# Self-products of batch rows: two adjacent rows to a partition, five long pieces a row, and paired product rows in one VectorE instruction

## The chip, the cores and the metric

The kernel runs on one core of a Trainium2 chip; the other cores are idle. The metric is the device time of one execution in microseconds (us). Ten runs of the kernel before gave 1312.31 to 1312.87 us, with a median of 1312.55.

## What is computed

The input has 4096 batch rows of 256 float32 numbers. For each row the kernel writes the upper triangle of the outer product of the row with itself:

```python
dot = jnp.einsum('bi,bj->bij', inputs, inputs)
iu, ju = jnp.triu_indices(d)
return dot[:, iu, ju]
```

The triangle is written row by row: first x[0] times x[0:256], then x[1] times x[1:256], and so on down to x[255] times itself. In this text a *product row* i is x[i] times x[i:256], with 256 - i numbers. An output row has 256 x 257 / 2 = 32,896 numbers, or 131,584 bytes; the output has 538.97 MB, the input 4.19 MB. There is one multiplication for each number that is stored.

## The kernel before, in words

The batch rows lie on the 128 partitions. A *group* is 512 batch rows: four tiles (t = 0 to 3, `GROUP`) of 128 rows, so that partition p holds rows p, 128 + p, 256 + p and 384 + p of the group, and there are 8 groups. At the start SP issues eight loads of 512 KB (L61), one for each group; each brings 128 x 4 rows of 1 KB. The input stays on the chip.

The output row is cut at multiples of 128 columns into 16 pieces (`CHUNKS`, `chunk_borders`) of 2,048 columns, the last of 2,176. The outer loop runs over the groups (L64), the inner one over the pieces (L66). For each piece a tile `o` is taken from a pool of 4 buffers (L53, L67); it holds the piece for all four rows of a partition. `runs` lists the stretches of product rows that fall into the piece. A stretch of up to 64 numbers (`SHORT`) takes one tensor_tensor on VectorE for the four rows together (L71), whose second operand is the factor, repeated along the stretch. A longer stretch takes four instructions, one for each row: three tensor_scalar on VectorE (L86) and one activation on ScalarE (L84), with the factor as their scale. Then SP issues one store of the piece for the 512 rows (L87): 4 MB, in packets of 8,192 bytes, one for each row.

Every engine works through its queue in the order in which the program issues. The framework puts in the waits: the first writer of a tile waits until the store that last read this buffer has landed (all 16 DMA engines have added to its semaphore), and SP's store waits for the last instruction of VectorE and of ScalarE on the tile. Two writers of one tile that overlap are ordered as well: if they stand on one engine, the later one waits for a semaphore that the earlier one raises. In the kernel before no two instructions on one tile are ordered in this way. A DMA of 128 partitions is spread over 16 DMA engines, which work through their shares at their own pace. 7383 instructions are in the profile; instructions themselves come into the engines' queues through a DMA queue (q14 in the profile).

Of the kernel before, what the change touches and what calls it, by code (L numbers as in the profile page):

```python
# [1 line left out]

# [4 lines left out]

F32 = mybir.dt.float32
AF = mybir.ActivationFunctionType
ALU = mybir.AluOpType  # L10

P = 128
UNIT = 128      # columns: chunk borders are multiples of it, 512 bytes in HBM
CHUNKS = 16     # pieces that an output row is cut into
GROUP = 4       # batch tiles of 128 rows that are computed and stored together
SHORT = 64      # runs up to this length take one instruction for the whole group


def chunk_borders(width: int) -> list[int]:
    units = width // UNIT  # L20
    borders = [units * c // CHUNKS * UNIT for c in range(CHUNKS)]
    return borders + [width]


def runs(d: int, lo: int, hi: int):
    """The runs of output columns [lo, hi) with one first factor: (i, j, column, length), for
    x[i] * x[j : j + length]. Row i of the upper triangle has j from i on."""
    at = 0
    for i in range(d):
        a, b = max(at, lo), min(at + d - i, hi)  # L30
        if a < b:
            yield i, i + a - at, a, b - a
        at += d - i


@with_exitstack
def kernel(
    ctx: ExitStack, tc: tile.TileContext, x: bass.AP, out: bass.AP
):
    """out[n, :] = the upper triangle, row by row, of the outer product of x[n] with itself.  # L40

    Batch rows lie on the partitions. The input stays on chip; the output is made chunk by chunk
    and each chunk goes out in one store while the next ones are computed."""
    nc = tc.nc
    n, d = x.shape
    width = out.shape[1]
    assert n % (P * GROUP) == 0 and width == d * (d + 1) // 2 and width % UNIT == 0
    groups = n // (P * GROUP)
    borders = chunk_borders(width)
    widest = max(b - a for a, b in zip(borders, borders[1:]))  # L50

    xpool = ctx.enter_context(tc.tile_pool(name="x", bufs=1))
    opool = ctx.enter_context(tc.tile_pool(name="o", bufs=4))  # L53

    x_in = x.rearrange("(g t p) d -> g p t d", t=GROUP, p=P)
    x_out = out.rearrange("(g t p) c -> g p t c", t=GROUP, p=P)

    xs = []
    for g in range(groups):
        xt = xpool.tile([P, GROUP, d], F32, tag=f"x{g}", name=f"x{g}")  # L60
        nc.sync.dma_start(xt, x_in[g])  # L61
        xs.append(xt)

    for g in range(groups):  # L64
        xt = xs[g]
        for c, (lo, hi) in enumerate(zip(borders, borders[1:])):  # L66
            o = opool.tile([P, GROUP, widest], F32, tag="o", name=f"o_{g}_{c}")  # L67
            for i, j, col, length in runs(d, lo, hi):
                a = col - lo
                if length <= SHORT:  # L70
                    nc.vector.tensor_tensor(  # L71
                        o[:, :, a : a + length],
                        xt[:, :, j : j + length],
                        xt[:, :, i : i + 1].to_broadcast([P, GROUP, length]),
                        ALU.mult,
                    )
                    continue
                for t in range(GROUP):
                    dst = o[:, t, a : a + length]
                    src = xt[:, t, j : j + length]  # L80
                    factor = xt[:, t, i : i + 1]
                    # Of four such instructions one goes to the Scalar engine.
                    if t == GROUP - 1:
                        nc.scalar.activation(dst, src, AF.Copy, scale=factor)  # L84
                    else:
                        nc.vector.tensor_scalar(dst, src, factor, None, ALU.mult)  # L86
            nc.sync.dma_start(x_out[g][:, :, lo:hi], o[:, :, : hi - lo])  # L87


# [1 line left out]
_INS = ["r_inputs"]  # L91
_OUTS = [((4096, 32896), "float32")]


# [20 lines left out]
```

## Time and profile before

| What | Before |
|---|---|
| Time, median of 10 runs | 1312.55 us |
| Time of the profiled execution | 1312.31 us |
| Its span, first to last event | 1310.5 us |
| VectorE (DVE) busy | 1117.1 us, 5272 instructions |
| ScalarE (ACT) busy | 506.2 us, 1553 instructions |
| DMA, mean over the span | 415 GB/s |
| Stores | 120 of 4096 KB and 8 of 4352 KB |
| Median from issue to landing of a 4096 KB store | 31.5 us |
| Last compute instruction ends | 1287.9 us |

Busy time is the time in which at least one instruction of the engine was under way; instructions can overlap on an engine, so "mean ns of one" times the count can be more than the busy time. The slices divide the span into 40 equal parts; a digit is the busy share of a part in tenths. "Idle before" is the time for which an engine did nothing ahead of an instruction, with what ended that wait behind the arrow. A row of the table of stretches gives, for a stretch of the span in us, its length, the busy time and the number of instructions of VectorE, ScalarE and GpSimd, the granted clock, the mean busy share of the 16 DMA engines and the rate at which they moved bytes. A share can be slightly above 1, because packets of one DMA engine overlap.

### The profile page before, as it was taken

To read this page: it belongs to the slowest core of one execution; us is meant where nothing else is said; L and a number is where in the kernel's file an instruction comes from. 1 tells how busy PE (TensorE), PEld (TensorE's weight loads), DVE (VectorE), ACT (ScalarE), POOL (GpSimd) and SP (SyncE) were. 2 spreads that over 40 slices of the span, in tenths; PEclk is the share of its full clock that TensorE was granted. 3 is DMA by queue.
4 is the path that set the end of the run, shared out by engine and by line. 5 is a ranking of instruction groups with operands and counts; after the bars stand their busy time and mean duration, and the time that the engine had idled before them with its cause. 6 is when DMAs were issued, how large, how long until landed. Compare 5 with 4: busy or idle time off the path is not lost.

```text
span 1310.5 us, 7383 instructions
## 1 busy us (share of the span) xinstructions
DVE 1117.1 (85%) x5272; ACT 506.2 (39%) x1553; POOL 0.2 (0%) x4
## 2 busy tenths in 40 slices
DVE  8889977899788997789977899778996789977893
ACT  5345234442344523345333443334433443334430
POOL 0000000000000000000000000000000000000000
DMA  9999999999999999999999999999999999999996
GB/s 370 427 427 422 419 420 419 419 419 420 418 420 419 420 418 420 418 420 419 419 419 419 419 419 419 418 419 419 420 418 419 418 420 419 420 418 420 419 420 276
DMA packets 71865, 543.64 MB, mean 415 GB/s; under 512 B 2176, under 2 KB 6272, under 8 KB 6272
## 3 DMA queue, kind: packets, MB, share of 16 engines
q1 hardware_dynamic: 71808, 543.17, 100.0%
q14 instruction: 57, 0.47, 0.1%
HBM read 4.19 MB, written 538.97 MB: 414 GB/s over the span
## 4 chain that ended last, share of the span: by engine, by line
DMA 54%; DVE 43%; issue 0%; DVEq 0%; SPq 0%
DMA out_dram<-o 54%; DVE o L86 34%; DVE o L71 9%; DMA x<-in_r_inputs_dram 0%; DVEq L71 0%; SPq L87 0%; DVEq L86 0%; DVEq L111 0%
## 5 line engine op out<-in xcount | busy, mean ns | idle before, releaser
L86 DVE TENSOR_SCALAR o<-x 128x256 f32<-128x256 f32 (+44 forms) x4656 | 993.1, 329 | 110.6 <-DMA out_dram<-o 106.4
L84 ACT ACTIVATE o<-x 128x105 f32<-128x105 f32 (+59 forms) x1552 | 504.9, 416 | 762.7 <-DMA out_dram<-o 754.7
L71 DVE TENSOR_TENSOR o<-x 128x112 f32<-128x112 f32 (+51 forms) x616 | 141.4, 382 | 60.1 <-DMA out_dram<-o 60.1
L84 ACT ACT_TABLE_LOAD x1 | 1.3, 1283 | 0.7 <-PEq L102 0.7
L102 POOL MEMSET const-bfloat16-1.0<- 128x1 bf16 x1 | 0.1, 101 | 0.0
L102 POOL MEMSET const-uint8-127<- 128x1 uint8 x1 | 0.1, 101 | 0.0
L102 POOL MEMSET const-float32-0.0<- 128x1 f32 x1 | 0.1, 98 | 0.2 <-issue 0.2
L102 POOL MEMSET const-float32-1.0<- 128x1 f32 x1 | 0.1, 98 | 0.0
## 6 DMA issues: line engine op xcount, KB each, us to landing
out_dram<-o SPq DMA_DIRECT2D x120, 4096.0 KB, 31.5
out_dram<-o SPq DMA_DIRECT2D x8, 4352.0 KB, 22.6
x<-in_r_inputs_dram SPq DMA_DIRECT2D x8, 512.0 KB, 8.4
```

Of the source, the lines that this page charges most:

```text
L71: nc.vector.tensor_tensor(o[:, :, a : a + length], xt[:, :, j : j + length], xt[:, :, i : i + 1].to_broadcast([P, GROUP, length]), ALU.mult,)
L84: nc.scalar.activation(dst, src, AF.Copy, scale=factor)
L86: nc.vector.tensor_scalar(dst, src, factor, None, ALU.mult)
L102: nc = _bacc.Bacc("TRN2", target_bir_lowering=False, num_devices=1)
```

## The change

- **Rows and partitions.** Partition p now holds 32 adjacent batch rows, 32p to 32p + 31, in one input tile. It is loaded in three parts: the first two rows of every partition (256 KB), the rest of the first half, and the second half. The outer loop runs over 16 groups of two adjacent rows a partition (`REPEAT`), 256 batch rows in all.
- **Pieces.** The output row is cut into 5 pieces (`PIECES`) of 6,528 or 6,592 columns, at multiples of 64. A piece of two rows is a tile of 128 x 2 x 6,592 numbers, from a pool of 3 buffers. One store takes it out, 6.7 MB, one run of 26 KB for each row. The very first piece is cut in four (`FIRST`), each with a store of its own: 512, 1,024, 2,048 and 2,944 columns.
- **Instructions.** For a product row (or a stretch of one) there are three ways on VectorE: "each", one tensor_scalar for each of the two rows; "all", one tensor_tensor for both rows; "two", one tensor_tensor for both rows and two product rows that follow each other. In the last, the second product row is taken as long as the first, one number too long, and the number too many is overwritten by the product row after it. `vector_ops` chooses by a formula for the times.
- **Order.** `interleave` cuts VectorE's part of a piece in two halves and issues one instruction of either half in turn.
- **The split.** `split` gives the first product rows of a piece to ScalarE, one activation for each batch row, until VectorE's part fits in a budget of 1.08 ns for each number of a partition, or ScalarE has more to do than VectorE. In the first piece the budget is 0, so that the two engines share it by time.

The diff, with runs of empty lines closed up:

```diff
--- before.py
+++ after.py
@@ -10,81 +10,159 @@
 ALU = mybir.AluOpType
 
 P = 128
-UNIT = 128      # columns: chunk borders are multiples of it, 512 bytes in HBM
-CHUNKS = 16     # pieces that an output row is cut into
-GROUP = 4       # batch tiles of 128 rows that are computed and stored together
-SHORT = 64      # runs up to this length take one instruction for the whole group
+UNIT = 64
+REPEAT = 2
+PIECES = 5
+BUDGET = 1.08
+FIRST = [512, 1536, 3584]
 
 
-def chunk_borders(width: int) -> list[int]:
-    units = width // UNIT
-    borders = [units * c // CHUNKS * UNIT for c in range(CHUNKS)]
-    return borders + [width]
+def even_borders(lo: int, hi: int, pieces: int) -> list[int]:
+    units = (hi - lo) // UNIT
+    return [lo + units * c // pieces * UNIT for c in range(pieces)] + [hi]
 
 
-def runs(d: int, lo: int, hi: int):
-    """The runs of output columns [lo, hi) with one first factor: (i, j, column, length), for
-    x[i] * x[j : j + length]. Row i of the upper triangle has j from i on."""
-    at = 0
+def runs(d: int, lo: int, hi: int) -> list:
+
+    found, at = [], 0
     for i in range(d):
         a, b = max(at, lo), min(at + d - i, hi)
         if a < b:
-            yield i, i + a - at, a, b - a
+            found.append((i, i + a - at, a, b - a))
         at += d - i
+    return found
+
+def vector_ops(block: list) -> list:
+
+    ops, k = [], 0
+    while k < len(block):
+        i, j, at, n = block[k]
+        two = k + 2 < len(block) and i == j
+        each = REPEAT * (130 + 0.52 * n)
+        together = 68 + 1.046 * REPEAT * n - (34 if two else 0)
+        if each <= together:
+            ops.append(("each", block[k]))
+        elif two:
+            ops.append(("two", block[k]))
+            k += 1
+        else:
+            ops.append(("all", block[k]))
+        k += 1
+    return ops
+
+def interleave(block: list) -> list:
+
+    half, at = 0, sum(n for *_, n in block) / 2
+    while half < len(block) and at > 0:
+        at -= block[half][3]
+        half += 1
+    a, b = vector_ops(block[:half]), vector_ops(block[half:])
+    return [op for k in range(max(len(a), len(b))) for ops in (a, b) for op in ops[k : k + 1]]
+
+def vector_time(block: list) -> float:
+    t = 0.0
+    for way, (i, j, at, n) in vector_ops(block):
+        if way == "each":
+            t += REPEAT * (130 + 0.52 * n)
+        else:
+            t += 68 + 1.046 * REPEAT * n * (2 if way == "two" else 1)
+    return t
+
+def split(block: list, budget: float) -> int:
+
+    scalar, k = 0.0, 0
+    while k < len(block):
+        scalar += REPEAT * (184 + 0.837 * block[k][3])
+        if vector_time(block[k:]) <= budget or scalar > vector_time(block[k + 1 :]):
+            break
+        k += 1
+    return k
+
+def window(ap: bass.AP, free: list) -> bass.AP:
+    return bass.AP(ap.tensor, ap.offset, [list(ap.ap[0]), *free])
 
 
 @with_exitstack
 def tile_self_products_kernel(
     ctx: ExitStack, tc: tile.TileContext, x: bass.AP, out: bass.AP
 ):
-    """out[n, :] = the upper triangle, row by row, of the outer product of x[n] with itself.
 
-    Batch rows lie on the partitions. The input stays on chip; the output is made chunk by chunk
-    and each chunk goes out in one store while the next ones are computed."""
+
     nc = tc.nc
     n, d = x.shape
     width = out.shape[1]
-    assert n % (P * GROUP) == 0 and width == d * (d + 1) // 2 and width % UNIT == 0
-    groups = n // (P * GROUP)
-    borders = chunk_borders(width)
-    widest = max(b - a for a, b in zip(borders, borders[1:]))
+    assert n % (P * REPEAT) == 0 and width == d * (d + 1) // 2 and width % UNIT == 0
+    groups = n // (P * REPEAT)
+    borders = even_borders(0, width, PIECES)
+    slot = max(b - a for a, b in zip(borders, borders[1:]))
 
     xpool = ctx.enter_context(tc.tile_pool(name="x", bufs=1))
-    opool = ctx.enter_context(tc.tile_pool(name="o", bufs=4))
+    opool = ctx.enter_context(tc.tile_pool(name="o", bufs=3))
 
-    x_in = x.rearrange("(g t p) d -> g p t d", t=GROUP, p=P)
-    x_out = out.rearrange("(g t p) c -> g p t c", t=GROUP, p=P)
+    x_in = x.rearrange("(p r) d -> p (r d)", p=P)
+    x_out = out.rearrange("(p g r) c -> g p r c", p=P, r=REPEAT)
 
-    xs = []
-    for g in range(groups):
-        xt = xpool.tile([P, GROUP, d], F32, tag=f"x{g}", name=f"x{g}")
-        nc.sync.dma_start(xt, x_in[g])
-        xs.append(xt)
+
+    total = n // P * d
+    xt = xpool.tile([P, total + 1], F32, name="x")
+    nc.vector.memset(xt[:, total:], 0.0)
+    cuts = [0, REPEAT * d, total // 2, total]
+    for a, b in zip(cuts, cuts[1:]):
+        nc.sync.dma_start(xt[:, a:b], x_in[:, a:b])
 
     for g in range(groups):
-        xt = xs[g]
         for c, (lo, hi) in enumerate(zip(borders, borders[1:])):
-            o = opool.tile([P, GROUP, widest], F32, tag="o", name=f"o_{g}_{c}")
-            for i, j, col, length in runs(d, lo, hi):
-                a = col - lo
-                if length <= SHORT:
+            o = opool.tile([P, REPEAT, slot], F32, tag="o", name=f"o_{g}_{c}")
+            first = g == c == 0
+            cuts = [lo, *(FIRST if first else []), hi]
+            for a, b in zip(cuts, cuts[1:]):
+                block = runs(d, a, b)
+                k = split(block, 0.0 if first else BUDGET * REPEAT * (b - a))
+                for i, j, at, length in block[:k]:
+                    for r in range(REPEAT):
+                        row = (g * REPEAT + r) * d
+                        nc.scalar.activation(
+                            o[:, r, at - lo : at - lo + length],
+                            xt[:, row + j : row + j + length],
+                            AF.Copy,
+                            scale=xt[:, row + i : row + i + 1],
+                        )
+                row = g * REPEAT * d
+                for way, (i, j, at, length) in interleave(block[k:]):
+                    at -= lo
+                    if way == "each":
+                        for r in range(REPEAT):
+                            row_r = row + r * d
+                            nc.vector.tensor_scalar(
+                                o[:, r, at : at + length],
+                                xt[:, row_r + j : row_r + j + length],
+                                xt[:, row_r + i : row_r + i + 1],
+                                None,
+                                ALU.mult,
+                            )
+                        continue
+                    m = 2 if way == "two" else 1
                     nc.vector.tensor_tensor(
-                        o[:, :, a : a + length],
-                        xt[:, :, j : j + length],
-                        xt[:, :, i : i + 1].to_broadcast([P, GROUP, length]),
+                        o[:, :, at : at + m * length].rearrange("p r (m l) -> p r m l", m=m),
+                        window(xt[:, row + j :], [[d, REPEAT], [1, m], [1, length]]),
+                        window(xt[:, row + i :], [[d, REPEAT], [1, m], [0, length]]),
                         ALU.mult,
                     )
-                    continue
-                for t in range(GROUP):
-                    dst = o[:, t, a : a + length]
-                    src = xt[:, t, j : j + length]
-                    factor = xt[:, t, i : i + 1]
-                    # Of four such instructions one goes to the Scalar engine.
-                    if t == GROUP - 1:
-                        nc.scalar.activation(dst, src, AF.Copy, scale=factor)
-                    else:
-                        nc.vector.tensor_scalar(dst, src, factor, None, ALU.mult)
-            nc.sync.dma_start(x_out[g][:, :, lo:hi], o[:, :, : hi - lo])
+                nc.sync.dma_start(x_out[g][:, :, a:b], o[:, :, a - lo : b - lo])
 
 
 # ---- launch: one core; inputs and outputs as the reference has them ----
```

## The prediction

> **What bounds the kernel now.** I read the page first: busy time, the forty slices, the DMA queues, the costliest groups.
>
> ```profile
> DVE 1117.1 (85%) x5272; ACT 506.2 (39%) x1553; POOL 0.2 (0%) x4
> ...
> DMA  9999999999999999999999999999999999999996
> GB/s 370 427 427 422 419 420 419 419 419 420 418 420 419 420 418 420 418 420 419 419 419 419 419 419 419 418 419 419 420 418 419 418 420 419 420 418 420 419 420 276
> ...
> q14 instruction: 57, 0.47, 0.1%
> ...
> L86 DVE TENSOR_SCALAR o<-x 128x256 f32<-128x256 f32 (+44 forms) x4656 | 993.1, 329 | 110.6 <-DMA out_dram<-o 106.4
> L71 DVE TENSOR_TENSOR o<-x 128x112 f32<-128x112 f32 (+51 forms) x616 | 141.4, 382 | 60.1 <-DMA out_dram<-o 60.1
> ```
>
> The 16 DMA engines are busy in every slice but the last, and VectorE's idle time ends with the landing of a store: it waits for buffers. The stores bound the kernel, at 428 GB/s early and 419 for the rest. Then the busy time per stretch, at both ends:
>
> ```profile
> 5.00:10.00 5.00, 5.00 (x21) 5.00 (x14) 0.00 (x0) 1.00 0.97 319
> ...
> 20.00:100.00 80.00, 71.30 (x320) 32.78 (x98) 0.00 (x0) 1.00 1.01 428
> ...
> 140.00:1280.00 1140.00, 983.01 (x4633) 442.03 (x1358) 0.00 (x0) 1.00 1.01 419
> ...
> 1300.00:1305.00 5.00, 0.00 (x0) 0.00 (x0) 0.00 (x0) 1.00 0.08 33
> 1305.00:1310.50 5.50, 0.00 (x0) 0.00 (x0) 0.00 (x0) 1.00 0.05 21
> ```
>
> The last two columns are the share of the DMA engines and GB/s. For the last 10 us the share is about 1/16: one engine of sixteen is late and alone sets the end. The landing records say the same: the lag of the last of 16 engines grows from 2 us to 10-12 us. I put it down to the 57 instruction packets of 8 KB: 7383 instructions to 57 packets is 130 a packet, VectorE's 5404 in the program fill 42, and 36 store packets took about 655 ns, twice the usual 316. 42 x 0.24 us = 10 us.
>
> Last, the timeline, for the price of one VectorE instruction:
>
> ```profile
> 4.12 6.35 DVE L86 TENSOR_SCALAR o<-x 128x256 f32<-128x256 f32 x24 [4.12 <-DMA x<-in_r_inputs_dram]
> ...
> 55.45 0.29 DVE L71 TENSOR_TENSOR o<-x 128x128 f32<-128x128 f32 x1 [2.24 <-DMA out_dram<-o]
> ...
> 65.24 0.33 DVE L71 TENSOR_TENSOR o<-x 128x164 f32<-128x164 f32 x1 [2.08 <-DMA out_dram<-o]
> ...
> 1274.65 13.21 DVE L71 TENSOR_TENSOR o<-x 128x256 f32<-128x256 f32 x64
> ```
>
> In a row, 64 tensor_tensor of together 8,320 elements take 13.21 us: 68 ns + 1.04 ns an element from start to start. Alone, 128 and 164 elements last 0.29 and 0.33 us: 158 ns + 1.04 an element. So the next one starts some 90 ns before its forerunner's recorded end. A tensor_scalar costs 129 ns + 0.52 an element (23 starts in 6.0 us at 252 elements).
>
> **What the Trainium skill says.** "DMA: Bandwidth & Descriptors", Why small descriptors are slow: a fixed overhead per packet; the trace agrees in kind, see the packet law below. The same page, Latency and other measured facts: a pitch of 4 MiB between partitions halved the rate of HBM copies and 4 KiB more restored it; no run here shows such a pitch. "Perfetto Trace Analysis", Per-engine timelines: the recorded end includes the acknowledgement of the writes, while the next instruction may start its prefetch earlier; the 90 ns agree. "VectorE: DVE Perf Modes", The DRAIN you can't avoid: a semaphore after each instruction cost nothing extra. That test added increments; for a wait on the instruction just ahead the trace argues otherwise.
>
> **The change, part by part.**
>
> *Stores.* Per row and piece, 2,048 columns (8,192 B, 65,536 packets) become about 6,579 (26.3 KB, some 20,500 packets). At 419.4 GB/s an 8 KB packet takes 8,192 x 16 / 419.4 = 312.5 ns on its engine. The loads' 1 KB packets moved 319 GB/s at a share of 0.97, or 49.8 ns. A line through both is 12 ns + 0.0367 ns/B, and gives 431 GB/s at 26.3 KB. The packet records of 8,704 B against 8,192 B (335 and 316 ns) give a steeper slope, 0.038, hardly a fixed part, and 420.5. I take 425, near the middle, and keep both ends. 538.97 MB at 425 is 1268 us.
>
> *Loads.* 4.19 MB in packets of 2 to 16 KB at 428 instead of about 330 GB/s: 9.8 us; from 2.1 us on they end at 11.9, against about 15 now. The first store needs only 512 columns, so it is queued behind the loads in time.
>
> *Instructions and the late engine.* The built program has 3,034 VectorE instructions instead of 5,404: 24 packets for 42, and the late engine lags 24 x 0.24 = 5.7 us, not 10.
>
> *VectorE.* It gets 1,326 tensor_scalar of 310,574 elements (171 + 161 us) and 1,635 tensor_tensor of 648,150 (111 + 674): 1118 us, as now. ScalarE falls to 786 instructions, about 231 us at 184 ns + 0.84 an element: it can bind nothing. But waits are added. Overlapping writes (a pair of rows writes one column too many) are ordered, and the interleaving was to put a stranger between them. In the built order 1,071 waits on VectorE's own semaphore name the instruction directly ahead: the tracker orders tiles by their whole interval over both batch rows. Behind such a wait stands all of VectorE's queue, then SP's store. Its price is not in the trace; bounded: the end of the forerunner (158 + 1.04n), 11 ns to the semaphore (the records of VectorE's own updates), and from there to the start 25 ns, as at the first instruction after its load landed, or 123 ns, as where a wait instruction of its own stands ahead. Less the 68 of the unhindered sequence: 126 or 224 ns. From below, zero, if the wait is met anyway. I take 126, since 1,055 of the waits sit on the instruction itself: 135 us. VectorE then needs 1118 + 135 = 1253 us for 1268 us of stream. The cover is thin: of five pieces the last three have 236, 345 and 429 such waits in 16 groups, so 15.9, 16.8 and 17.5 us a piece against 15.9 of stream; the first two (13.5 and 14.5) pay it back.
>
> *Three buffers, larger.* A piece may be computed while one store runs and one waits. In the first group there is no lead yet, and stores 3 and 5 come late by some 4 us in sum (the chain of VectorE reaches piece 5 at about 78, the DMA wants it at 76).
>
> *The sum.* 11.9 + 1268 + 4 + 5.7 + 0.5 (last landing) = 1290 us of span. VectorE's own chain: 4.1 to the first data + 1253 + 8 (64 separate waits of about 0.1, and others) + 18 for the last store = 1283, below it. The profiled execution took 1312.31 for a span of 1310.5, so 1.8 more: 1292 us. The median of the runs, 1312.55, is 0.24 above that one execution.
>
> **The rivals.**
>
> *The chain of waits becomes the bound (slower).* VectorE-bound, the span is 1148 + 1.071 us for each ns of a wait. From 154 ns on that passes 1313.4, which is slower by over 0.2%; at the middle between 126 and 224, 175 ns, 1335 and so 1337 us; at 224, 1390. For it: 1,071 waits in a row, and a margin of 15 us. Against: the wait is on the instruction itself, where 25 ns was seen.
>
> *Packet length doesn't pay.* If the 7 ns more than early (309 to 316 in the records) grow with bytes, the stream stays at 419 to 420.5: 1282 to 1285, in sum 1304 to 1307 of span, 1306 to 1309 us. For it: the 8,704 B packets. Against: the 1 KB loads.
>
> *All of it is per packet, and waits cost little.* 431 GB/s: 1250.5 + 11.9 + 3 + 5.7 + 0.5 = 1272, or 1273 us.
>
> *The pitch.* Partitions are now 32 x 131,584 B apart, 4 MiB + 16 KiB, where 131,584 B stood. By the skill the odd KiB should save it. A rate under 417 is already slower than before: (1313.4 - 22) us for 538.97 MB.
>
> **How the numbers follow.** Forecast (1276 to 1304 us) 0.58; chain of waits from 154 ns on 0.18; length doesn't pay 0.12; all per packet 0.05; pitch 0.07. About 0.2% is what a measurement of this kernel can tell from no change. Faster: 0.58 + 0.05 + 0.09 of the second rival + 0.02 of the first at its lower edge = 0.74; within: 0.07; slower: 0.19. The range runs from the 1272 of the per-packet case to the 1337 of the chain at 175 ns; outside lie about 0.07 of the chain, 0.05 of the pitch and 0.02 below.
>
> **What would show it.** GB/s of 425 in the slices from the fourth on; 1 KB packets gone, and a last stretch with a share of 1/16 that lasts 5 to 6 us; VectorE's idle time named by its own semaphore, some 130 us, and starts of tensor_tensor 194 ns + 1.04 an element apart; little left of its waits for stores. Wrong it would be with DMA slices under 9 in the middle (VectorE-bound), or with a rate of 419 or less at full share.

## The result, and the profile after

The changed kernel takes 1283.36 us (median of 8 runs, 1283.29 to 1283.49), against 1312.68 us for the kernel before in the same sessions: a ratio of 0.9776, 95% interval 0.9768 to 0.9785, or 29.3 us less. The profiled execution has a span of 1281.6 us. The forecast was 1292, with a range of 1272 to 1337.

The page of the changed kernel, the same parts as were shown of before and the shares of the chain that ended last:

```profile
DVE 1219.2 (95%) x2962; ACT 235.4 (18%) x787; POOL 0.2 (0%) x4
...
DMA  9999999999999999999999999999999999999999
GB/s 383 405 395 432 422 432 435 421 432 422 432 422 422 433 422 432 435 419 423 433 431 425 426 428 422 432 434 421 422 427 427 435 420 434 422 433 422 432 422 395
...
q14 instruction: 32, 0.26, 0.1%
...
DVE 95%; issue 3%; DVEq 0%
DVE o L159 69%; DVE o L150 26%; DVEq L159 0%
...
L159 DVE TENSOR_TENSOR o<-x 128x2 f32<-128x2 f32 (+51 forms) x1635 | 915.3, 573 | 37.7 <-DVE o L159 0.5
...
L150 DVE TENSOR_SCALAR o<-x 128x216 f32<-128x216 f32 (+6 forms) x1326 | 366.2, 355 | 3.5 <-DMA x<-in_r_inputs_dram 2.4
```

(The chain that ended last is the work followed back from the last instruction to what released it each time.) In the kernel before, its shares were:

```profile
DMA 54%; DVE 43%; issue 0%; DVEq 0%; SPq 0%
```

Two readings. The rate has risen from 419 to some 427 GB/s. And VectorE no longer waits for a single store: of 166.5 us of such idle time nothing is left, and the chain that ended last runs through VectorE for 95% of the span, and no longer through the stores. VectorE has become the bound, though the DMA slices are all 9: here a DMA queue that is only just fed looks as busy as one that is full.

The stretches of the changed kernel (length, busy time and count of VectorE, ScalarE, GpSimd, clock, DMA share, GB/s):

```profile
5.00:10.00 5.00, 5.00 (x22) 5.00 (x14) 0.00 (x0) 1.00 1.02 429
...
20.00:100.00 80.00, 78.11 (x196) 14.21 (x48) 0.00 (x0) 1.00 0.95 407
...
140.00:1255.00 1115.00, 1080.39 (x2629) 198.97 (x672) 0.00 (x0) 1.00 1.00 427
...
1260.00:1265.00 5.00, 0.99 (x6) 0.00 (x0) 0.00 (x0) 1.00 1.00 427
...
1275.00:1281.60 6.60, 0.00 (x0) 0.00 (x0) 0.00 (x0) 1.00 0.61 260
```

From 5 to 10 us, while the loads run, the rate is 429 GB/s instead of 319. Between 20 and 100 us the stream falls to 407: the first group, in which VectorE has no lead. At the end there is no stretch with 1/16 of the engines: in the landing records the 16 engines of a store land within 1.9 us of each other from the first store to the last. That fits an engine that catches up whenever the queue runs short; in experiments 2 and 3 below, where VectorE is held up too, they stay within 1.7 us, and in the kernels with multiplications whose stream is the bound (before, and experiments 1, 4 and 5) one engine falls behind by 7 us or more.

Last, single forms of line 159 in the changed kernel (busy us and mean ns of one, idle us before them, all of one form together):

```profile
L159 DVE TENSOR_TENSOR o<-x 128x804 f32<-128x804 f32 x16 | 16.0, 999 | 0.5
...
L159 DVE TENSOR_TENSOR o<-x 128x360 f32<-128x360 f32 x32 | 17.1, 534 | 1.1
```

804 elements last 999 ns, 360 last 534: within 5 ns of 158 ns + 1.04 an element, the time of an instruction alone. The idle time ahead is 0.5 us for 16, 1.1 us for 32, or 34 ns each. So they follow each other at 192 ns + 1.04 an element, not at the 68 of the unhindered sequence: 124 ns for a wait, where 126 was forecast. As an instruction counts as busy until its recorded end, most of this shows as busy time (1219 us, where the unhindered sum is 1118) and only 37.7 us of it as idle time. The waits can be counted in the trace: 1,070 of VectorE's instructions start within 100 ns after the end of the one ahead, 34 ns in the median; the others start before that end, or after a longer pause (17 of them).

### The profile page after: what moved, and what is told of

It reads as the page before. It is cut to its first block, busy times and chain, and to the rows that moved or that the text cites. A ratio compares the mean times of both kernels' runs of the same rounds, so it can differ in the third digit from the quotient of the medians.

```text
span 1281.6 us, 4091 instructions
## 1 busy us (share of the span) xinstructions
DVE 1219.2 (95%) x2962; ACT 235.4 (18%) x787; POOL 0.2 (0%) x4
## 3 DMA queue, kind: packets, MB, share of 16 engines
HBM read 4.19 MB, written 538.97 MB: 424 GB/s over the span
## 4 chain that ended last, share of the span: by engine, by line
DVE 95%; issue 3%; DVEq 0%
DVE o L159 69%; DVE o L150 26%; DVEq L159 0%
## 5 line engine op out<-in xcount | busy, mean ns | idle before, releaser
L159 DVE TENSOR_TENSOR o<-x 128x2 f32<-128x2 f32 (+51 forms) x1635 | 915.3, 573 | 37.7 <-DVE o L159 0.5
L138 ACT ACTIVATE o<-x 128x197 f32<-128x197 f32 (+25 forms) x786 | 234.1, 390 | 1005.3 <-DMA out_dram<-o 778.6
L150 DVE TENSOR_SCALAR o<-x 128x216 f32<-128x216 f32 (+6 forms) x1326 | 366.2, 355 | 3.5 <-DMA x<-in_r_inputs_dram 2.4
L138 ACT ACT_TABLE_LOAD x1 | 1.3, 1283 | 0.7 <-PEq L180 0.7
```

What stands on the lines that cost most here:

```text
L138: nc.scalar.activation(o[:, r, at - lo : at - lo + length], xt[:, row + j : row + j + length], AF.Copy, scale=xt[:, row + i : row + i + 1],)
L150: nc.vector.tensor_scalar(o[:, r, at : at + length], xt[:, row_r + j : row_r + j + length], xt[:, row_r + i : row_r + i + 1], None, ALU.mult,)
L159: nc.vector.tensor_tensor(o[:, :, at : at + m * length].rearrange("p r (m l) -> p r m l", m=m), window(xt[:, row + j :], [[d, REPEAT], [1, ...
```

## The experiments

My theory after the result: VectorE's waits on the instruction directly ahead set the end, and the stream by itself would allow less. The rival: the stream sets it, and the waits lie beside it.

**1. The same instructions, another view of the output.** Most of the waits come from how the output of line 159 is written: through a rearranged view, which by the prediction is tracked as one interval over both batch rows. This run writes it as a plain slice.

```diff
-                        o[:, :, at : at + m * length].rearrange("p r (m l) -> p r m l", m=m),
+                        o[:, :, at : at + m * length],
```

> The changed kernel with the output of the tensor_tensor written as a plain slice instead of a rearranged view: same instructions and operands, but only 304 instead of 1,071 of VectorE's waits on itself name the instruction directly ahead. Theory (VectorE's chain of waits sets the end): VectorE sheds some 767 x 124 ns = 95 us, waits for stores again, and the time falls to what the stream allows, 1275 to 1279 us. Rival (the stream of stores already sets the end, the waits lie beside it): within 1 us of 1283.4.

Measured: 1277.72 us (0.9732 of before, 0.9717 to 0.9746), 5.6 less than the changed kernel. The shares of the chain that ended last, and the two groups of VectorE:

```profile
DMA 54%; DVE 43%; issue 1%; DVEq 0%; SPq 0%
...
L159 DVE TENSOR_TENSOR o<-x 128x660 f32<-128x660 f32 (+50 forms) x1635 | 831.8, 574 | 66.5 <-DMA out_dram<-o 56.0
...
L150 DVE TENSOR_SCALAR o<-x 128x225 f32<-128x225 f32 (+5 forms) x1326 | 347.9, 344 | 22.8 <-DMA out_dram<-o 20.1
```

The waits of this run (engine and line, for whom, us in total, times, longest):

```profile
DVE o L159 <- DMA out_dram<-o: 56.0, 41, 2.1
DVE o L150 <- DMA out_dram<-o: 20.1, 13, 1.6
```

and its stretches:

```profile
20.00:100.00 80.00, 79.35 (x211) 14.17 (x48) 0.00 (x0) 1.00 1.01 433
100.00:1200.00 1100.00, 1017.16 (x2609) 198.41 (x672) 0.00 (x0) 1.00 1.00 430
...
1265.00:1270.00 5.00, 0.00 (x0) 0.00 (x0) 0.00 (x0) 1.00 0.47 200
1270.00:1275.00 5.00, 0.00 (x0) 0.00 (x0) 0.00 (x0) 1.00 0.05 21
```

VectorE waits for stores again, 76 us, the stream runs at 430, the chain that ended last runs mostly through the stores, and the late engine is back at the end. A tensor_tensor lasts as long as before (574 and 573 ns in the mean), but only 304 instructions are left with a gap of some 34 ns ahead. Busy time and idle time other than for stores and loads fall from 1258 to 1165 us in sum: 93 us for 767 waits, or 122 ns each. The theory holds: with most of the waits gone the stream is the bound, and it ends 5.6 us before VectorE's chain did.

**2. Without the interleaving.**

```diff
-                for way, (i, j, at, length) in interleave(block[k:]):
+                for way, (i, j, at, length) in vector_ops(block[k:]):
```

> The changed kernel without the interleaving of the two halves of a piece: 1,193 waits on the instruction directly ahead instead of 1,071. Theory (chain of waits sets the end): up to 122 x 124 ns = 15 us more, 1290 to 1298 us. Rival (stream sets the end): within 1 us of 1283.4.

Measured: 1296.26 us, 12.9 more than the changed kernel for 122 more waits, 106 ns each. The edit also pairs the rows a little differently, with 32 instructions fewer (1,603 tensor_tensor for 1,635); at the 68 ns that one costs unhindered they would save 2.2 us, and with these the price is 124 ns a wait, by this estimate. What is added to the chain arrives at the end nearly whole: the rival is out.

**3. Less work for VectorE.**

```diff
-BUDGET = 1.08
+BUDGET = 1.0
```

> The changed kernel with a budget of 1.00 instead of 1.08: 86 us of multiplications move from VectorE (1118 to 1031) to ScalarE (226 to 372). Theory A (VectorE's own chain is the whole of it): VectorE ends well ahead, the stream sets the end, 1275 to 1279 us. Theory B (the view by whole intervals also orders ScalarE's and VectorE's writes to one piece, so that VectorE waits for ScalarE's longer share): slower, 1300 to 1320 us.

Measured: 1319.74 us, 1.0052 of the kernel before (1.0037 to 1.0066). Taking 86 us of work from the engine that is the bound costs 36 us. One of its waits, which the changed kernel doesn't have:

```profile
DVE o L159 <- ACT o L138: 138.2, 46, 6.7
```

ScalarE and VectorE touch no common number. But if the rearranged view counts as everything between its first and its last byte, a tensor_tensor over both batch rows covers ScalarE's share of the second row too, and waits for ScalarE. Theory A falls, and B has the sign and the size right; the next run tests whether it is the view.

**4. Both.** The plain slice and the budget of 1.00.

> Plain output slice and budget of 1.00 together. If the stream sets the end once the waits are gone, 1275 to 1279 us, as with the plain slice alone; if VectorE still sets it there, some 5 us or more below the plain slice alone.

Measured: 1276.33 us (0.9721 of before, 0.9705 to 0.9737), the fastest kernel of this study: 7.0 us below the changed one, 36.6 below the one before in its session. Its waits for stores:

```profile
DVE o L159 <- DMA out_dram<-o: 114.3, 45, 3.5
DVE o L150 <- DMA out_dram<-o: 46.9, 20, 3.6
```

Against experiment 1 it is only 1.4 less, with VectorE's waits for stores at 161 us instead of 76: the stream is the bound in both. Against experiment 3 the one edit of the view is worth 43.4 us, and no wait of VectorE for ScalarE is left. That shows the view as the cause of the waits on ScalarE too. How the framework compares the bytes behind a view is not shown by these runs; they show that the waits come with the view and go with the plain slice.

**5. No pairs.** Is the pairing of product rows, from which the overlaps come, worth having?

```diff
-        two = k + 2 < len(block) and i == j
+        two = False
```

> The changed kernel with the pairing of product rows switched off: every tensor_tensor takes one product row. No two writes of VectorE overlap, so none of its instructions waits on another; VectorE has 1113 us of work as before the edit, ScalarE 393 instead of 226, and VectorE's instructions go from 2,961 to 4,545. If the waits alone kept the changed kernel from the stream's time: 1278 to 1281 us (the stream's 1277 and up to 3 us for 12 more instruction packets on the late engine). If the pairing itself was worth something: slower than 1283.

Measured: 1286.90 us, 3.5 more than the changed kernel, not 2 to 5 less. VectorE waits for stores (125 us), the stream runs at 430, and no instruction of VectorE is left with a gap of some 34 ns ahead: the waits are gone and the stream is the bound. The end shows what was missed:

```profile
1265.00:1270.00 5.00, 0.00 (x0) 0.00 (x0) 0.00 (x0) 1.00 0.66 285
1270.00:1275.00 5.00, 0.00 (x0) 0.00 (x0) 0.00 (x0) 1.00 0.09 37
1275.00:1280.00 5.00, 0.00 (x0) 0.00 (x0) 0.00 (x0) 1.00 0.06 26
1280.00:1285.00 5.00, 0.00 (x0) 0.00 (x0) 0.00 (x0) 1.00 0.04 16
```

For 15 us one DMA engine of sixteen is still at work. In the landing records of the last store 13 engines end within 0.2 us, one 15.7 us after the first; in experiment 1 that is 7.6. The first engine is only 1.0 us later than in experiment 1, so 8.1 of the 9.2 us between the two are the late engine. There are 48 instruction packets instead of the 32 of the changed kernel and of experiment 1, 16 more and not 12. The pairing is worth its fewer instructions, not its VectorE time, if it is the instruction packets that make the engine late; experiment 7 tests that.

**6. The stores alone.** Five kernels with no loads and no multiplications, only the stores of resident buffers, in two row layouts and three packet lengths. Their stream starts only after the buffers have been filled, at 37 us with 8 KB packets, 42 with 26 KB and 47 with 44 KB, so the rates are compared between lengths, not the times. The core of the edit, against the changed kernel:

```diff
-            for a, b in zip(cuts, cuts[1:]):
-                block = runs(d, a, b)
...
+            o = os[k % BUFS]
+            nc.vector.memset(o[:, :, 0:1], float(k))
+            nc.sync.dma_start(x_out[g][:, :, lo:hi], o[:, :, : hi - lo])
```

> Stores alone, loads and multiplications left out: rows, pieces and buffers as in the kernel before (8 KB packets, 128 rows between a partition's rows). 419 to 421 GB/s in the middle slices if the stream by itself is what the kernel before ran at; no engine late at the end, since there are hardly any instructions.

> Stores alone, loads and multiplications left out: adjacent rows, but 8 KB packets of 4 rows and 4 buffers. If only packet length matters, 419 to 421 GB/s as in the kernel before; if the new row layout helps or hurts by itself, another rate.

> Stores alone: loads and multiplications are left out (one column of a buffer is set before each store). Rows, pieces and buffers as in the changed kernel: 26 KB packets, adjacent rows. If the packet law holds half way (some 8 ns a packet), 428 to 431 GB/s in the middle slices; if length doesn't pay, 419 to 421; if the pitch of 4 MiB + 16 KiB hurts, below 417.

> Stores alone, loads and multiplications left out: 26 KB packets in the row layout of the kernel before (128 rows between a partition's two rows). If only the packet's length matters, 430 GB/s as with adjacent rows; if the pitch of 4 MiB + 16 KiB costs something at this length, more than 431.

> Stores alone, loads and multiplications left out: one row a partition and store, in three pieces of 44 KB. By the packet law (12 to 14 ns a packet and 0.0367 ns a byte) 432 GB/s in the middle slices, 2 more than with 26 KB; if the gain ends at some length, 430.

Measured, in the same stretch of each run (length, VectorE, GpSimd, clock, share, GB/s). 8 KB in the rows of before:

```profile
100.00:1200.00 1100.00, 6.76 (x109) 0.00 (x0) 1.00 1.01 419
```

8 KB in adjacent rows:

```profile
100.00:1200.00 1100.00, 6.76 (x109) 0.00 (x0) 1.00 1.01 419
```

26 KB in adjacent rows:

```profile
100.00:1200.00 1100.00, 4.20 (x70) 0.00 (x0) 1.00 1.00 430
```

26 KB in the rows of before:

```profile
100.00:1200.00 1100.00, 4.20 (x70) 0.00 (x0) 1.00 1.00 430
```

and 44 KB in adjacent rows:

```profile
100.00:1200.00 1100.00, 5.01 (x85) 0.00 (x0) 1.00 1.00 432
```

Within one length the times can be compared too: 1327.77 and 1327.78 us for the two layouts at 8 KB, 1300.77 and 1300.76 at 26 KB. The 44 KB run starts its stream last and still ends first, at 1299.29. The layout is worth nothing, the length of the packet what there is. It isn't the number of stores: there are 128 at 8 KB, 80 at 26 KB, and 96 at 44 KB, which is faster with more of them. 8,192 bytes at 419 GB/s are 313 ns an engine, 26,317 at 430 are 979, 43,861 at 432 are 1624: about 12 ns a packet and 0.0367 ns a byte to within 3 ns, the line of the prediction drawn from 1 KB and 8 KB.

**7. Instructions as packets.** The 8 KB stores in the rows of before, with 5,248 tiny VectorE instructions added, in two placements. First 41 after each store, on a tile of their own:

```diff
-EXTRA = 0
+EXTRA = 41
...
             for e in range(EXTRA):
                 nc.vector.memset(busy[:, e % 8 : e % 8 + 1], float(e))
```

Then 41 ahead of each store, on its buffer:

```diff
-            nc.sync.dma_start(x_out[g][:, :, lo:hi], o[:, :, : hi - lo])
             for e in range(EXTRA):
-                nc.vector.memset(busy[:, e % 8 : e % 8 + 1], float(e))
+                nc.vector.memset(o[:, e % 4, 1 + e // 4 : 2 + e // 4], float(e))
+            nc.sync.dma_start(x_out[g][:, :, lo:hi], o[:, :, : hi - lo])
```

> The run of the kernel before's stores alone with 5,248 tiny VectorE instructions added (41 after each store), which touch none of the stores' buffers. Theory (instruction packets delay one DMA engine): 41 more packets of 8 KB, 10 us more than without them, and a last stretch of 10 us with a DMA share of about 1/16. Rival (the late engine has another cause): no difference over 1 us.

> Stores alone of 8 KB packets, loads and multiplications left out, with 5,248 tiny VectorE instructions as before, but 41 of them ahead of each store on its buffer, so that they are spread over the whole run and not bunched at its start. Theory A (each instruction packet costs the late engine some 0.24 us, as worked out from the kernel before; bunching made it 0.5): 10 us over the 1327.8 us of the run without them. Theory B (it is the number of such instructions, however placed): 20 to 23 us over it.

Measured: 1350.57 us in the first placement, 22.8 over the run without them; 1339.92 in the second, 12.2 over it. In the first, the framework moved the tiny instructions forward, up to 219 between two stores, and the last of them ran at 316 us; in the second, each 41 wait for a buffer and are spread over the run. Both have 45 instruction packets instead of 4. The end of the run without them, where all engines are busy together until it is over:

```profile
1310.00:1320.00 10.00, 0.00 (x0) 0.00 (x0) 1.00 1.01 422
1320.00:1330.00 10.00, 0.00 (x0) 0.00 (x0) 1.00 0.41 173
```

The end of the spread run:

```profile
1325.00:1330.00 5.00, 0.00 (x0) 0.00 (x0) 1.00 0.09 36
1330.00:1335.00 5.00, 0.00 (x0) 0.00 (x0) 1.00 0.06 26
1335.00:1338.20 3.20, 0.00 (x0) 0.00 (x0) 1.00 0.04 16
```

One engine is late by 12 us, with hardly any computation in the kernel. In the landing records of the last store one engine comes 11.8 us after the first, where that is 0.7 without the tiny instructions. In the bunched run this lag has grown to 21 us by the store that lands at 271 us, and after the last tiny instruction it no longer grows. The packet records show where the time goes: in the spread run 40 of the 8 KB store packets took over 500 ns, 655 in the median, where 314 is usual, and 39 of the 45 instruction packets ran at the same time as one of these. It is the instruction packets that delay the engine. 12.2 us for 41 packets are 0.30 us each when spread, 0.56 when bunched. Theory A was right on the placement and 2 us low. Why a packet costs more when they are bunched was not settled.

## Why the prediction was right, and where it was wrong

- *The sum.* 1292 was forecast, 1283.4 measured, inside the range and on the right side, at 1.4 times the forecast gain. The error is 8.6 us, and not all of one kind: a stream that was put 15 us too long stood first in the sum, and the second sum, VectorE's, set the end. That the number came out as near as it did rests on the two sums having been 7 us apart.
- *The stream's rate: the step that failed.* "I take 425, near the middle": the stores alone run at 430, and so does the stream where VectorE's waits are gone. The line through 1 KB and 8 KB gives 978 ns for a 26 KB packet, where 979 were measured. The other end came from packets of 8,704 against 8,192 bytes, which differ by 19 ns; 1 ns more or less in that difference moves the fixed part of a packet by 16 ns. And the reading doesn't follow from its own two durations: 335 and 316 ns give 0.0371 ns a byte and a fixed part of 12 ns, the first line again, and not 0.038 and hardly any. It should not have had half the weight. In the sum the term is 1268 where 538.97 MB at 430 is 1253: 15 us too much. That the changed kernel runs at 427, close to the 425, is chance: that is the pace at which VectorE feeds the stores.
- *Which sum ends last.* With 1253 the stream's sum is 1275, below VectorE's own chain of 1283. So the kernel ended on the chain: the prediction had it as the second sum, at 1283 of span against a measured 1281.6. The forecast named the stream as the bound; it is VectorE, by 5.6 us (experiment 1). The slower rival named the right mechanism; it stayed harmless because the price was 124 ns, well below the 154 from which it would have made the kernel slower.
- *The price of a wait.* 126 forecast, 124 from the trace, 122 in experiment 1, 106 in experiment 2 before its fewer instructions are allowed for. Right, and it rested on the lone instructions and on a release after 25 ns. The signs given for it were partly wrong: most of the time is not idle time with VectorE's name (0.5 us has it), but busy time that has grown.
- *The first group.* 4 us forecast; 80 us at 407 instead of 430 are 4.3 us. The time belongs to VectorE's waits: in experiment 1 the same stretch runs at 433.
- *The loads.* 429 GB/s from 5 to 10 us against the 428 assumed, but the last load packet ended at 13.7 us, where 11.9 was forecast. As VectorE is the bound, this does not reach the end.
- *The late engine.* 5.7 us forecast; no more than 1.9 in the changed kernel. It comes back where the stream is the bound: 7.6 us between the first and the last engine in experiment 1, 15.7 in experiment 5. The cause, only argued then, is shown by experiment 7; the size of 0.24 us a packet was low, 0.30 when spread there, and 0.5 for each of the 16 more packets of experiment 5.
- *The pitch.* No cost: 430 in either layout. That rival is out at both packet lengths.
- *Where VectorE would be the bound, "DMA slices under 9".* Wrong: it is the bound with slices of 9 and a share of 1.00. What told it apart was that VectorE waits for no store, and the chain that ended last.

The remark of the Trainium skill, "VectorE: DVE Perf Modes", The DRAIN you can't avoid, that a semaphore after each instruction costs nothing extra, doesn't carry over to this case: what costs here is a wait on the instruction directly ahead, 124 ns in each of 1,071.

What stays open: why both full kernels stream 1 to 2% faster in their first 100 us (428 and then 419 before; 433 and then 430 in experiment 1) than the stores alone at any time (419; 430 to 431).

## What to carry to other kernels

Look in the built program for waits of an engine on its own semaphore before trusting a rate measured without them: two instructions that touch no common number can still be ordered, if the output is handed to the framework through a rearranged view, and then even moving work to an engine with time to spare can cost (36 us here). A store-bound kernel like this one gains from longer packets, in either of the two row layouts, though little beyond 26 KB (419, 430 and 432 GB/s at 8, 26 and 44 KB). The number of instructions counts even where VectorE waits for stores, because instruction packets share the DMA engines with the stores: 1,584 more instructions of VectorE and 576 of ScalarE cost most of the 9.2 us between experiments 1 and 5. Where two sums end within 1% of each other, forecast both, since a few GB/s decide which one is last.

## What was not expected of the hardware

- Instruction packets delay mainly one of the sixteen DMA engines: it ended 15.7 us after the first in experiment 5, with 13 others within 0.2 us, and lost 0.30 to 0.56 us for each packet of 8 KB in experiment 7.
- The cost of a store packet follows one line from 8 to 44 KB: 12 ns and 0.0367 ns a byte on each engine.
- A distance of 4 MiB + 16 KiB between partitions in HBM changed nothing: 1300.76 us against 1300.77.
